# Moving the back transforms, the sums and the feed-forward within the two-row steps of a window-attention and Fourier kernel

## The chip, the cores and the metric

The kernel runs on one core of a Trainium2 chip. The metric is the device time of the whole kernel in microseconds: 3787.6 us before the change, the median of three runs (3779.0 to 3789.97). All data are float32.

## What is computed

Two layers on 32 images of 56 x 56 tokens with 128 channels. Each layer adds a branch of the group-normalised image to the image:

```python
x = x + window_attention(gn(x))     # 7x7 windows, shifted by 3, 4 heads, relative bias and mask
x = x + feedforward(fourier(gn(x)))
# fourier: along rows and along columns, cosine transform, keep 32 modes,
#          one 128x128 matrix per mode, transform back; the two results are added
# feedforward: relu(h @ W1 + b1) @ W2 + b2, 128 -> 512 -> 128
```

`gn` takes mean and variance over a whole image for each group of 4 channels, so the second layer of an image starts when its attention is over.

## The kernel before

**Image and rows.** An image has 8 rows of windows (`NWR`), of 8 windows with 49 tokens each. After the first 8 rows, which run one by one (`first_rows`), everything runs in `step(g)`, which takes two rows: `cur` are the rows 2g and 2g+1, `prev` the two before them. An image thus takes four steps (`STEPS`), and 32 images take 128 steps and a tail.

**A step's attention.** For `cur`: queries and keys (`attn_qk`, L322 to L342), scores (`attn_scores`: 16 matmuls of each row into two PSUM banks, L376, then two additions of bias and mask on VectorE, L384), maximum and subtraction (`attn_max`, L394 and L395), values of the tokens (`attn_v`, L354 and L361), exponential (`attn_exp`, L401). For `prev`, in the step after: sums and division (`attn_divide`, L406 to L409), transposes of the weights on TensorE (`attn_transpose`, L420: two banks for each row, the first copied to `aT` by VectorE, L430, the second by ScalarE, L428), weights times values (`attn_values`, L445, two banks, copied by L476 on VectorE and L478 on ScalarE), projection and residual (`attn_project`, L487 and L495, written to the scratch tensor `scr`). `attn_sums` takes the sums for the second normalisation of the rows before those: first L509 on VectorE, and after its `yield` the squares on ScalarE (L517) and their sums on VectorE (L518).

**A step's second layer.** Image b enters it at step g = 4b + 5 (`CONV_BEGIN` = 5), and d counts its steps from there. `fourier(g)` lists the images at work with their d: two of them, the newest at d = 0 to 3 and the one before at d = 4 to 7.
- d = 0: statistics (`fourier_stats`: L529 adds up all sums of the image on VectorE, L538 is a matmul on them, L546 to L569 are small operations on VectorE with one on GpSimd, L567), all four forward transforms along the width and two along the height (`transform`, L596 and L604).
- d = 1: two more along the height, the modes of the width (`mix`, L630, L638, through the DRAM scratch `zscr`).
- d = 2: the modes of the height; transform back along the width, four groups of 16 lines (the last has 8) (`load_modes`, then `modes_back`: L669 into two banks, copied by L680 on ScalarE and VectorE).
- d = 3: transform back along the height, four groups; here both banks are added to `xf` by VectorE (L685).
- d = 4 to 7 (`FF_BEGIN` = 4): feed-forward, eight groups of 384 tokens (the last has 448), two in a step. `ff_in` loads the residual, multiplies by W1 (L717, four banks) and takes the relu on ScalarE (L725, `hid`), `ff_out` multiplies by W2 (L737) and adds the residual on VectorE (L746).

**The next image** is brought in meanwhile: `image_group` (eight of them; L260 on TensorE, L270 on ScalarE, L271 on VectorE, L275 on GpSimd): three before the transposes of the step with d = 1, three at its end and two at the beginning of the step with d = 2. `image_norm`, a generator in four pieces, takes the statistics of the next image (L282 to L313), with small matmuls (L285, L298, L311), VectorE in between (L291, L293, L300, L304) and GpSimd for the power (L302). Its second matmul, L298, is in the step with d = 2 ahead of the transposes.

**Order.** The body is built under `tc.manual_schedule(engines={PE, Activation, DVE, Pool})`: each of these four engines takes its instructions in the order in which the program writes them down. What an instruction waits for, across engines, is worked out from the tiles that it touches. Two PSUM pools of four banks each go round: `pa` for attention, `image_group`, `image_norm` and `fourier_stats`, `pc` for transforms, modes and feed-forward. An allocation takes the bank that was given out four allocations earlier, so the first matmul into it waits for the copy out of it.

Of the kernel before, what the change touches and what calls it, by code (L numbers as in the profile page):

```python
# [41 lines left out]
FF_GROUPS = (3 * P,) * 7 + (7 * JP,)  # L42
# [5 lines left out]
def swin_fourier_kernel(  # L48
# [564 lines left out]
    def load_columns(im, g):  # L613

        t = work.tile([TC, CH, C], F32, tag="htok", name="htok", bufs=2)
        src = im.scr.rearrange("h (n r) c -> r h n c", r=2)
        for r in range(2):
            nc.sync.dma_start(t[r * S : (r + 1) * S], src[r, :, CH * g : CH * (g + 1)])
        im.cols[g] = t
# [28 lines left out]
    def load_modes(im, width, g):  # L648
        l0, n = LINES[g]
        zT = work.tile([P, 4, C], F32, tag="zT", name="zT", bufs=4)  # L650
        nc.sync.dma_start(
            zT[:, : n // 4],
            im.zscr[width][l0 : l0 + n].rearrange("(m r) u k c -> (r u k) m c", r=4),
        )
        im.zT[width, g] = zT
# [120 lines left out]

    images = {}
    STEPS = NWR // 2
    FF_BEGIN = 4

    def row(r):
        return (images[r // NWR], r % NWR) if 0 <= r < NB * NWR else (None, 0)
# [4 lines left out]
    def fourier(g):  # L787

        b, d = divmod(g - CONV_BEGIN, STEPS)
        return [(images[b - k], d + k * STEPS) for k in (1, 0) if 0 <= b - k < NB]  # L790

    first_done = set()

# [4 lines left out]
    def step(g):  # L798
        prev, cur, b, i = rows(g - 1), rows(g), *divmod(g, STEPS)
        conv = fourier(g)  # L800
        following = images.get(b + 1)

        def groups(js):
            if following:
                for j in js:
                    image_group(following, j)

        norm = None
        if following and i == STEPS - 1:
            norm = image_norm(following)  # L810


        if i == STEPS - 1:
            groups((6, 7))
        if norm:
            next(norm)
        for im, d in conv:
            if d >= FF_BEGIN:
                ff_in(im, 2 * (d - FF_BEGIN))
        for im, j, r in prev:  # L820
            if once("divide", r):
                attn_divide(r)
        sums = []
        for im, j, r in rows(g - 2):
            if once("sums", r):
                sums.append(attn_sums(im, j))
                next(sums[-1])
        for im, j, r in cur:
            attn_qk(im, j, r, False)
        if norm:  # L830
            next(norm)
        for k in sums:
            next(k)
        for im, d in conv:
            if d == 0:
                im.stats = fourier_stats(im)
                im.cols = {}
                next(im.stats)
                load_columns(im, 0)
                load_columns(im, 1)  # L840
            if d in (2, 3):
                for k in range(len(LINES)):
                    load_modes(im, d == 2, k)
        for im, d in conv:
            if d >= FF_BEGIN:
                ff_out(im, 2 * (d - FF_BEGIN))
                ff_in(im, 2 * (d - FF_BEGIN) + 1)
        for im, d in conv:
            if d == 0:
                next(im.stats)  # L850
        if norm:
            next(norm)
        if i == STEPS - 2:
            groups((0, 1, 2))
        for im, j, r in prev:
            attn_transpose(im, j, r)


        for im, j, r in prev[:1]:
            attn_values(im, j, r)  # L860


        for k in range(2):
            for im, d in conv:
                if d in (2, 3):
                    modes_back(im, d == 2, k)
        for im, j, r in cur:
            attn_scores(im, j, r)
        for k in range(2, 4):
            for im, d in conv:  # L870
                if d in (2, 3):
                    modes_back(im, d == 2, k)
        for im, j, r in cur:
            attn_max(r)


        for im, d in conv:
            if d == 0:
                for k in range(4):
                    transform(im, True, k)  # L880
            if d in (0, 1):
                for k in (2 * d, 2 * d + 1):
                    transform(im, False, k)
                    if d == 0:
                        load_columns(im, k + 2)
            if d in (1, 2):
                for k in range(4):
                    mix(im, d == 1, k)
        for im, j, r in cur:
            attn_v(im, j, r)  # L890


        for im, j, r in prev[1:]:
            attn_values(im, j, r)


        for im, j, r in cur:
            attn_exp(r)
        for im, d in conv:
            if d >= FF_BEGIN:  # L900
                ff_out(im, 2 * (d - FF_BEGIN) + 1)
        for im, j, r in prev:
            attn_project(im, j)
        if i == 1 and b + 1 < NB:
            images[b + 1] = image_begin(b + 1)
        if i == STEPS - 2:
            groups((3, 4, 5))
        if norm:
            next(norm)
# [125 lines left out]
```

## Time and profile before

| | before |
|---|---|
| device time, us | 3787.6 (3779.0 to 3789.97) |
| span of the profiled execution, us | 3778.7 |
| TensorE matmul: busy | 3612.5 us, 96% |
| TensorE weight load: busy | 3055.2 us, 81% |
| VectorE: busy | 2280.0 us, 60% |
| ScalarE: busy | 2155.6 us, 57% |
| GpSimd: busy | 1366.0 us, 36% |
| share of TensorE in the chain that ended last | 84% |
| DMA: mean rate | 103 GB/s |

Busy time is the time in which an engine executes. A matmul of float32 counts twice here, since it is executed as two passes; the end of a matmul is modelled. In the profile's lines, "pa<-aT,v" says that `pa` is written and `aT` and `v` are read; what stands after "<-" in brackets or in the wait view released the engine from its idle time. `L420` is line 420 of the kernel. PE is TensorE, PEld its weight load, ACT ScalarE, DVE VectorE, POOL GpSimd.

### The profile page before, as it was taken

To read this page: it belongs to the slowest core of one execution; us is meant where nothing else is said; L and a number is where in the kernel's file an instruction comes from. 1 tells how busy PE (TensorE), PEld (TensorE's weight loads), DVE (VectorE), ACT (ScalarE), POOL (GpSimd) and SP (SyncE) were. 2 spreads that over 40 slices of the span, in tenths; PEclk is the share of its full clock that TensorE was granted. 3 is DMA by queue.
4 is the path that set the end of the run, shared out by engine and by line. 5 is a ranking of instruction groups with operands and counts; after the bars stand their busy time and mean duration, and the time that the engine had idled before them with its cause. 6 is when DMAs were issued, how large, how long until landed. Compare 5 with 4: busy or idle time off the path is not lost.

```text
span 3778.7 us, 140104 instructions
## 1 busy us (share of the span) xinstructions
PE 3612.5 (96%) x61696; PEld 3055.2 (81%) x61696; DVE 2280.0 (60%) x4739; ACT 2155.6 (57%) x3913; POOL 1366.0 (36%) x1453
## 2 busy tenths in 40 slices
PE   7899999999999999999999999999999999999999
PEld 5788888888887888888888788878888888888887
DVE  6766566665665656665656656566566666565641
ACT  5565555655555555556555565555555555555553
POOL 5343333433333333333333333333343333333321
PEclk9999999999999999999999999999999999999999
DMA  4343333434434344344433343443444333434333
GB/s 111 93 112 99 98 94 101 120 98 111 106 92 105 96 114 105 92 106 117 98 97 104 93 118 99 113 101 92 105 102 114 98 100 102 114 98 104 95 105 96
DMA packets 688417, 388.93 MB, mean 103 GB/s; under 512 B 41120, under 2 KB 658753, under 8 KB 687553
## 3 DMA queue, kind: packets, MB, share of 16 engines
q1 hardware_dynamic: 687197, 379.65, 38.8%
q8 instruction: 485, 7.95, 0.9%
q14 instruction: 124, 1.01, 0.1%
q10 hardware_dynamic: 611, 0.32, 0.0%
HBM read 218.29 MB, written 161.48 MB: 101 GB/s over the span
## 4 chain that ended last, share of the span: by engine, by line
PE 84%; DVE 7%; ACT 4%; issue 3%; SPq 1%; DMA 1%; POOL 0%; ACTq 0%; DVEq 0%; POOLq 0%
PE pc L737 18%; PE pc L717 15%; PE pc L630 6%; PE pc L596 6%; PE pa L354 6%; PE pa L376 5%; PE pa L487 5%; PE pa L445 5%; PE pc L669 4%; PE pa L329 4%; PE pa L322 4%; PE pa L420 3%; ACT hid L725 2%; PE pa L260 2%; DVE st L271 1%
## 5 line engine op out<-in xcount | busy, mean ns | idle before, releaser
L725 ACT ACTIVATE hid<-pc,b1sb 128x384 f32<-128x384 f32 (+1 forms) x1024 | 600.3, 587 | 610.4 <-PE pc L717 557.2
L737 PE MATMUL pc<-wff,hid 128*128 128x128 f32 x6400 | 783.3, 278 | 8.0 <-issue 7.3
L737 PEld LDWEIGHTS pc<-wff,hid 128*128 128x128 f32 x6400 | 745.4, 190 | 52.6 <-issue 8.7
L717 PE MATMUL pc<-xf,wff 128*128 128x384 f32 (+1 forms) x2048 | 727.0, 496 | 19.8 <-DVE res L746 19.8
L395 POOL TENSOR_TENSOR a<-a,mx 128x784 f32<-128x784 f32 x256 | 383.8, 1520 | 1000.0 <-DVE mx L394 906.9
L409 POOL TENSOR_TENSOR a<-a,rs 128x784 f32<-128x784 f32 x256 | 383.6, 1521 | 611.7 <-ACT hid L725 369.2
L717 PEld LDWEIGHTS pc<-xf,wff 128*128 128x128 f32 x2048 | 367.0, 190 | 243.9 <-DVE res L746 37.7
L476 DVE TENSOR_SCALAR oT<-pa,bqkv 128x98 f32<-128x98 f32 (+2 forms) x768 | 171.1, 278 | 500.9 <-PE pa L445 500.9
L275 POOL TENSOR_TENSOR xl<-xl,bproj 112x384 f32<-112x384 f32 (+1 forms) x256 | 291.3, 1141 | 282.0 <-PE pa L260 277.1
L746 DVE TENSOR_TENSOR res<-pc,res 128x384 f32<-128x384 f32 (+1 forms) x288 | 148.1, 523 | 375.6 <-PE pc L737 208.5
L707 POOL TENSOR_TENSOR res<-res,b2sb 128x384 f32<-128x384 f32 (+1 forms) x288 | 270.4, 944 | 263.3 <-DMA res<-scr 254.9
L604 ACT ACTIVATE y<-pc,rstd 128x448 f32<-128x448 f32 x256 | 167.5, 655 | 195.6 <-PE pc L596 189.7
L384 DVE TENSOR_TENSOR a<-pa,bm 128x392 f32<-128x392 f32 x512 | 256.2, 558 | 36.1 <-PE pa L376 31.4
L361 ACT COPY v<-pa 128x512 f32<-128x512 f32 x256 | 147.8, 589 | 201.8 <-PE pa L354 201.3
L376 PE MATMUL pa<-k,q 64*64 64x98 f32 x8192 | 231.4, 248 | 32.7 <-issue 27.8
L445 PE MATMUL pa<-aT,v 49*32 49x49 f32 x16384 | 208.7, 212 | 49.5 <-DVE aT L430 40.2
L354 PE MATMUL pa<-wn,xw 128*64 128x128 f32 x4096 | 250.2, 274 | 2.8 <-DVE a L384 2.8
L401 ACT ACTIVATE a<-a 128x784 f32<-128x784 f32 x256 | 210.8, 864 | 70.1 <-POOL a L395 70.1
L342 DVE TENSOR_SCALAR k<-pa,heads,bqkv 128x392 f32<-128x392 f32 x248 | 169.2, 684 | 134.8 <-ACT k L334 134.8
L445 PEld LDWEIGHTS pa<-aT,v 49*32 49x32 f32 x16384 | 174.5, 105 | 89.1 <-ACT aT L428 50.8
L376 PEld LDWEIGHTS pa<-k,q 64*64 64x64 f32 x8192 | 200.5, 132 | 50.4 <-issue 36.6
L406 DVE TENSOR_REDUCE sm<-a 128x16 f32<-128x784 f32 x256 | 238.1, 930 | 4.4 <-ACT a L401 4.4
(90 smaller groups left out, 5903.3 us busy)
## 6 DMA issues: line engine op xcount, KB each, us to landing
zscr<-z SPq DMA_DIRECT2D x512, 112.0 KB
htok<-scr SPq DMA_DIRECT2D x256, 196.0 KB
res<-scr SPq DMA_DIRECT2D x256, 192.0 KB
zT<-zscr SPq DMA_DIRECT2D x192, 256.0 KB
out_dram<-res SPq DMA_DIRECT2D x224, 192.0 KB
scr<-xl SPq DMA_DIRECT2D x128, 224.0 KB
xl<-in_x_dram SPq DMA_DIRECT2D x32, 784.0 KB
xl<-in_x_dram SPq DMA_DIRECT2D x32, 672.0 KB
```

Of the source, the lines that this page charges most:

```text
L275: nc.gpsimd.tensor_tensor(piece, piece, bproj.unsqueeze(1).to_broadcast([TC, n1 - n0, C]), ALU.add)
L354: nc.tensor.matmul(pv[hs, j * C : (j + 1) * C], lhsT=im.xw[i][:, w * WT : w * WT + JP], rhs=im.w[:, 2 * C : 3 * C], start=True, stop=True,)
L376: nc.tensor.matmul(ps[hp][HALVES[e], pr * 2 * WT : (pr + 1) * 2 * WT], lhsT=q[cs, w * WT : w * WT + JP], rhs=k[cs, :, w], start=True, stop ...
L384: nc.vector.tensor_tensor(a[:, 2 * hp : 2 * hp + 2, :, 0:WT].rearrange("p u w j -> p w u j"), ps[hp][:, :RT].rearrange("p (w u j) -> p w u ...
L395: nc.gpsimd.tensor_tensor(a3, a3, mx.unsqueeze(2).to_broadcast([P, 2 * NWR, WT]), ALU.subtract)
L406: nc.vector.tensor_reduce(sm, a3, axis=AX.X, op=ALU.add)
L409: nc.gpsimd.tensor_tensor(a3, a3, rs.unsqueeze(2).to_broadcast([P, 2 * NWR, WT]), ALU.mult)
L445: nc.tensor.matmul(po4[u][h * HD : (h + 1) * HD, 2 * f + e], lhsT=v[ks, 2 * f + e, h * HD : (h + 1) * HD], rhs=im.aT[i][f][ks, h, e * JP : ...
L707: nc.gpsimd.tensor_tensor(res[:m, c0:c1], res[:m, c0:c1], b2sb[:m].unsqueeze(1).to_broadcast([m, c1 - c0, C]), ALU.add,)
L717: nc.tensor.matmul(ph[:, :n], lhsT=wff1[:, f * P : (f + 1) * P], rhs=xff[:, t0 : t0 + n], start=True, stop=True,)
L725: nc.scalar.activation(hf[:, :n], ph[:, :n], AF.Relu, bias=b1sb[:, f : f + 1])
L737: nc.tensor.matmul(pf[:m, c * C : (c + 1) * C], lhsT=im.hid[f][:, c * P : c * P + m], rhs=wff2[:, f], start=(f == 0), stop=(f == NF - 1),)
```

## The change

All of it is in the planning of the steps; no operation is added or taken out.

1. The transforms back are spread over four steps instead of two: two groups at each of d = 2 and 3 for the width and d = 4 and 5 for the height. One group stands ahead of the scores of `cur`, one behind them; before, two stood on each side.
2. The values of the first row of `prev`, which followed the transposes directly, follow the scores and the second group back, so that matmuls that do not depend on the copies of the transposes lie between.
3. The feed-forward begins at d = 6 instead of 4, since the transforms back now end at d = 5. Three images can be in the second layer at once, and the last two steps of one run beside the first two of the image after the next one.
4. The DMA loads of a step (columns of `scr` at d = 0, modes at d = 2 to 5) are issued ahead of the feed-forward in the middle of the step.
5. `ff_out` and the second `ff_in` stand ahead of the second half of `attn_sums` (`next(k)`: L517 and L518); before, they stood behind it.
6. The statistics at d = 0: the sum L529 still follows the second half of `attn_sums`, and so follows the feed-forward now; the second half (L538 and after) stands behind the transposes instead of before them.

```diff
-    FF_BEGIN = 4
+    FF_BEGIN = 6
...
-        return [(images[b - k], d + k * STEPS) for k in (1, 0) if 0 <= b - k < NB]
+        return [
+            (images[b - k], d + k * STEPS)
+            for k in (2, 1, 0)
+            if 0 <= b - k < NB and d + k * STEPS < FF_BEGIN + len(FF_GROUPS) // 2
+        ]
...
+        for im, d in conv:
+            if d == 0:
+                im.cols = {}
+                load_columns(im, 0)
+                load_columns(im, 1)
+            if 2 <= d < FF_BEGIN:
+                for k in range(2):
+                    load_modes(im, d < 4, d % 2 * 2 + k)
+        for im, d in conv:
+            if d >= FF_BEGIN:
+                ff_out(im, 2 * (d - FF_BEGIN))
+                ff_in(im, 2 * (d - FF_BEGIN) + 1)
         for k in sums:
             next(k)
         for im, d in conv:
             if d == 0:
                 im.stats = fourier_stats(im)
-                im.cols = {}
-                next(im.stats)
-                load_columns(im, 0)
-                load_columns(im, 1)
-            if d in (2, 3):
-                for k in range(len(LINES)):
-                    load_modes(im, d == 2, k)
-        for im, d in conv:
-            if d >= FF_BEGIN:
-                ff_out(im, 2 * (d - FF_BEGIN))
-                ff_in(im, 2 * (d - FF_BEGIN) + 1)
-        for im, d in conv:
-            if d == 0:
                 next(im.stats)
...
         for im, j, r in prev:
             attn_transpose(im, j, r)
+        for im, d in conv:
+            if d == 0:
+                next(im.stats)
+
+        def back(k):
+            for im, d in conv:
+                if 2 <= d < FF_BEGIN:
+                    modes_back(im, d < 4, d % 2 * 2 + k)
+
+        back(0)
+        for im, j, r in cur:
+            attn_scores(im, j, r)
+        back(1)
 
         for im, j, r in prev[:1]:
             attn_values(im, j, r)
-
-        for k in range(2):
-            for im, d in conv:
-                if d in (2, 3):
-                    modes_back(im, d == 2, k)
-        for im, j, r in cur:
-            attn_scores(im, j, r)
-        for k in range(2, 4):
-            for im, d in conv:
-                if d in (2, 3):
-                    modes_back(im, d == 2, k)
         for im, j, r in cur:
             attn_max(r)
```

## The prediction

> **What bounds the kernel now.** I read the totals first, then the waits of TensorE, then one image's four steps as windows, then those steps engine by engine in the timeline.
>
> The totals of the page:
>
> ```profile
> PE 3612.5 (96%) x61696; PEld 3055.2 (81%) x61696; DVE 2280.0 (60%) x4739; ACT 2155.6 (57%) x3913; POOL 1366.0 (36%) x1453
> ```
>
> TensorE sets the time: 166 of 3778.7 us are left. The granted clock was 0.996. No reordering can win more than those 166 us, and it can lose any amount, since a TensorE idle for lack of an operand has nothing to make it up with. The wait view of TensorE says what they are (engine line waited for: us in total, times, longest us):
>
> ```profile
> PE pa L445 <- DVE aT L430: 40.2, 61, 1.4
> PE pa L376 <- issue: 27.8, 37, 1.6
> PE pc L717 <- DVE res L746: 19.8, 29, 0.7
> ...
> PE pc L630 <- ACT xf L680: 4.2, 19, 0.2
> ```
>
> The attention values (L445) wait for the transposed weights; L717, on 29 steps, for a bank that L746 empties. "issue" is time for which the profile shows no partner. Now one image from the middle, one window a step (columns: stretch, length, busy time of PE, PEld, DVE, ACT, POOL, clock, DMA), each from the start of its transposes (L420):
>
> ```profile
> 1481.38:1510.04 28.66, 27.84 (x509) 23.93 (x509) 15.10 (x33) 17.90 (x33) 9.30 (x11) 1.00 0.61 129
> 1510.04:1540.65 30.61, 29.48 (x473) 25.27 (x471) 20.58 (x41) 18.75 (x35) 16.34 (x21) 1.00 0.33 95
> 1540.65:1569.20 28.55, 28.31 (x507) 24.01 (x506) 16.60 (x35) 17.55 (x34) 8.91 (x8) 1.00 0.40 116
> 1569.20:1594.60 25.40, 25.40 (x449) 21.32 (x448) 18.80 (x38) 12.89 (x23) 7.95 (x6) 1.00 0.32 82
> ```
>
> I call them steps 0 to 3, after d of the newest image. The idle time of TensorE in this image is 2.2 us: 0.82 and 0.46 before L445 in steps 0 and 1, 0.67 before L717 and 0.24 before L630. Step 3 has none. The timeline shows why (start, us, what):
>
> ```profile
> 1476.73 1.03 ACT L517 ACTIVATE sq<-xl 112x384 f32<-112x384 f32 x2
> 1479.53 2.52 ACT L725 ACTIVATE hid<-pc,b1sb 128x384 f32<-128x384 f32 x4 [1.78 <-PE pc L717]
> 1482.41 0.54 ACT L428 COPY aT<-pa 113x452 f32<-113x452 f32 x1 [0.36 <-PE pa L420]
> ```
>
> ```profile
> 1483.14 0.16 DVE L569 SCALAR_TENSOR_TENSOR shift<-ms,rstd 128x1 f32<-128x1 f32 x1 [0.66 <-POOL rstd L567]
> 1483.22 1.16 DVE L430 COPY aT<-pa 113x452 f32<-113x452 f32 x2
> ...
> 1505.07 1.14 DVE L518 TENSOR_REDUCE part<-sq 112x32 f32<-112x384 f32 x2
> 1506.48 0.56 DVE L746 TENSOR_TENSOR res<-pc,res 128x384 f32<-128x384 f32 x1 [0.28 <-issue]
> 1510.06 1.50 DVE L271 BATCH_NORM_STATS2 st<-xw 128x6 f32<-128x392 f32 x3 [3.02 <-ACT xw L270]
> 1511.48 1.15 DVE L430 COPY aT<-pa 113x452 f32<-113x452 f32 x2
> ```
>
> ```profile
> 1483.99 0.80 PE L445 MATMUL pa<-aT,v 49*32 49x49 f32 x64 [0.82 <-DVE aT L430]
> ```
>
> In step 0 VectorE's copy L430 stands behind the statistics (L546 to L569, 1481.58 to 1483.30), in step 1 behind three L271. The first copy ends at 1483.84, and L445 starts 0.15 later: my price of a hand-over to TensorE. Equally important: the squares L517 stand on ScalarE *before* the four relus (L725), in an idle stretch, and so L518 is over before the transposes begin. The last relu ends 0.84 us after the ff_in matmuls (1482.05 against 1481.21; the same in step 3, 1570.04 against 1569.20).
>
> **What the Trainium skill says.** "PSUM — Partial Sum Buffer", section "Engine vs sequencer instructions": the queues of ScalarE, VectorE and GpSimd are strict FIFO, and matmuls start in program order. The trace agrees: L430 of 1511.48 sat behind L271 although its transposes had begun at 1510.04. "Perfetto Trace Analysis", section "Identifying the Most-Contended Engine": matmul busy share is no good measure of closeness to the roofline. Here PEld, 81%, points to TensorE as well. Same page, "Optimization Strategy": a bubble that repeats can mean too few buffers for the next tile. That bears on what follows: the four transposes take all four `pa` banks, and the scores need two of them back.
>
> **The change, part by part.** Each engine's order is that of the program, so I place every instruction behind those ahead of it. T is when TensorE reaches the transposes, as it does now.
>
> *Removed.* Scores and one `modes_back` group now lie between transposes and values, so L445's old wait goes (40.2), L746 moves ahead of L518, so L717's goes (19.8), and only two groups stand ahead of `mix`, so L630's goes (4.2). Together 64 us.
>
> *Moved at no cost.* No TensorE work is added. Loads of zT are still issued a step or more after their writes. The feed-forward's delay keeps its two groups a step; softmax (L394 to L409) starts up to 4 us later, but its exp waits behind the second values on ScalarE anyway (L401 at T+13.1 in step 0) and its division ends more than 6 us before the next transposes.
>
> *Added: `next(k)` after the second ff_in.* It puts L517 behind the relus: last relu T+0.84, squares to T+1.87 (1.03), L518 to T+2.6 (its second takes 0.68 after the second square). The first copy L430 then ends at T+3.15 (0.62), and the second at T+3.7. Before, step 3's first copy ended at T+1.23. Transposes take 1.62 us of issue, one back group 0.85 (1.70 for two), a row's scores 0.88 (1.77 for two), two score additions 1.0 (1.99 for four).
> - Step 3: transposes to T+1.62, back(0) to 2.5. Scores need the bank of the first copy, 3.15+0.15 = 3.3: wait 0.8. Values find their two banks some 0.1 late. Together **0.85**.
> - Step 2: the norm's L300 and L304 stand behind L518 too. L300 at T+2.55 frees the bank of the last transpose, which has started by 1.2: wait 1.5. L304 follows 0.82 later (measured, through GpSimd's L302), the copy ends at 3.9, scores at 4.05 after back(0) to 3.95: 0.1. **1.6**.
> - Step 1: ff_in is over 1.23 earlier, but L270 (0.42 each) also stands behind the squares: it ends at 1.1, 1.5 and 1.9, and the last transposes end at 2.4 instead of 1.62: 0.8. Three L271 (1.5) then L430: first copy 3.4, scores 3.55 against back(0) to 3.25: 0.3. Additions end at 6.1, values are reached at 5.65: 0.6. **1.7**.
> - Step 0: the total L529 (0.69) follows L518, to T+3.2, and L538, now directly after the transposes, needs it: TensorE waits from 1.62 to 3.35, 1.7. Queued behind it are back(0), scores and everything else. Statistics end at 5.95 (chain of 1.72 after the copies), two additions of back(0) at 7.0 (1.11), scores' at 8.0. Values are reached at 6.9, start at 8.15: 1.25. **2.95**.
>
> Sum: 29 of steps 0 and 1 each, 30 of 2 and 3 have both attention and feed-forward: 29 x (2.95+1.7) + 30 x (1.6+0.85) = 208 us added. Net of the 64: +144.
>
> *Feed-forward two steps later.* Image 0 runs steps 0 and 1 once more without it. Its absence at 110 to 157 us shows waits of 1.26, 1.41 and 4.88, against 0.83, 0.46 and 0.67 with it: +5.6. At the end four more groups have nothing between ff_in and ff_out: L737 takes 3.17 there, 2.92 in the mean elsewhere, +1. Together +6.
>
> *Unknown: "issue".* It comes in clusters, at L376 above all. The trace does not say what it depends on. A wait ahead of the scores may cover it: between none and all 78 us that the clusters cost (the excess of all steps over their clean lengths); other arrangements of short matmuls could add 30. I take half of L376's: -14.
>
> 3787.6 + 144 + 6 - 14 = 3924.
>
> **Rivals.**
> 1. *Late copies, as above*: 3924, chance 0.6. For it: each term is a queue position times a measured duration. Against it: hand-built schedules of five queues leave room for a bank assigned otherwise.
> 2. *The same, but the new waits swallow the "issue" clusters, or a third of them fails to appear*: 144 becomes about 66 to 96: 3854 to 3890, chance 0.24. For: both are idle TensorE. Against: many clusters lie later in the step.
> 3. *As the order of matmuls suggests*: scores and back groups cover the copies fully, nothing new arises: -64 + 6 = 3730, chance 0.12. For: in step 3 of now, copies, two back groups and scores run with no wait. Against: there L518 was done 3 us before.
> 4. *Both cancel*: 3788, chance 0.04.
>
> **How the numbers follow.** Slower 0.84 (rivals 1 and 2), same 0.04, faster 0.12. The range goes from the lower half of rival 2 (3835, where half the L538 term fails besides) to 3970 (208 us in full, nothing of "issue" saved and 30 added: 3968).
>
> **What would show it.** L517 after L725 on ScalarE, with L518 ending 2 to 3 us after the transposes start; a wait of TensorE at L538 for L529, near 1.7 us in each step 0; waits of L376 for L430, near 0.8 in step 3; waits of L420 for L270 in step 1 and for L300 in step 2; L445 waiting for L384. The waits for L746 and L680 gone. I am wrong if L538 and L376 show no such waits, or if L517 runs between the relus and ends early.

## The result and the profile after

| | before | after |
|---|---|---|
| device time, us | 3783.3 (3778.67 to 3789.97, 4 runs) | 3849.78 (3845.89 to 3852.51, 4 runs) |
| span of the profiled execution, us | 3778.7 | 3850.2 |
| TensorE idle in the span, us | 166.2 | 204.4 |
| granted clock in the span | 0.996 | 0.992 |

The change makes the kernel slower: 1.0174 times the time before, with a 95% interval of 1.0151 to 1.0196. That is +66 us; the forecast was +136. The kernel moved to the side that the forecast named, but by about half of the distance.

The totals of the profile page after:

```profile
PE 3645.8 (95%) x61696; PEld 3078.4 (80%) x61696; DVE 2260.3 (59%) x4739; ACT 2143.3 (56%) x3913; POOL 1364.3 (35%) x1453
```

No engine has one instruction more, and TensorE's busy time is 33 us longer all the same. The other part of the 71.5 us by which the span grew is 38 us of idle time. The wait view of TensorE after:

```profile
PE pa L538 <- DVE tot L529: 52.0, 32, 3.1
PE pa L420 <- DVE ve L300: 30.4, 29, 1.1
PE pa L445 <- DVE a L384: 24.1, 71, 1.1
PE pa L445 <- issue: 17.0, 21, 2.0
PE pa L420 <- ACT xw L270: 13.4, 28, 0.7
...
PE pa L376 <- DVE aT L430: 7.5, 34, 1.0
```

Every new wait of the forecast is there with the releaser named in it: the statistics' matmul L538 for the total L529 (step 0), the transposes L420 for L300 (step 2) and for L270 (step 1), the values L445 for the additions L384 (steps 0 and 1), the scores L376 for the copy L430 (step 3). The three old waits (L445 for L430, L717 for L746, L630 for L680; 64 us together) are not in the view any more. The new ones are 52.0 + 30.4 + 24.1 + 13.4 + 7.5 = 127 us of idle time; the forecast said 208.

Windows of one image in the middle, after, as the prediction cut them, by the starts of L420: steps 0, 1 and 2, then the whole image (stretch, length, busy time of PE, PEld, DVE, ACT, POOL, clock, DMA):

```profile
1474.85:1507.54 32.69, 30.17 (x573) 25.59 (x572) 17.80 (x38) 18.02 (x33) 9.71 (x12) 1.00 0.53 115
1507.54:1540.28 32.74, 31.95 (x528) 27.48 (x527) 22.08 (x46) 18.59 (x36) 16.36 (x21) 1.00 0.31 90
1540.28:1568.25 27.97, 26.92 (x459) 22.95 (x458) 15.47 (x33) 16.35 (x33) 8.50 (x7) 1.00 0.35 102
1474.85:1591.43 116.58, 112.03 (x1929) 95.01 (x1928) 70.30 (x147) 66.45 (x123) 42.52 (x45) 1.00 0.40 102
```

Before, such an image took 113.22 us with 2.2 idle. Now it takes 116.58 with 4.55 idle: 2.52 of it in step 0 (first length minus first busy time), 0.79 in step 1, 1.05 in step 2. So two thirds of the loss in an image are idle time, and 1.0 us is longer busy time for the same matmuls.

Where the waits come from stands in the timeline of a step 0 (T = 1591.73, the start of the transposes). First ScalarE, then VectorE, then TensorE:

```profile
1590.06 2.52 ACT L725 ACTIVATE hid<-pc,b1sb 128x384 f32<-128x384 f32 x4 [2.71 <-PE pc L717]
1592.47 1.03 ACT L517 ACTIVATE sq<-xl 112x384 f32<-112x384 f32 x2
```

```profile
1593.02 1.20 DVE L518 TENSOR_REDUCE part<-sq 112x32 f32<-112x384 f32 x2 [3.06 <-ACT sq L517]
1594.26 0.69 DVE L529 TENSOR_REDUCE tot<-part 112x64 f32<-112x512 f32 x1
1594.86 1.16 DVE L430 COPY aT<-pa 113x452 f32<-113x452 f32 x2
...
1598.64 1.97 DVE L384 TENSOR_TENSOR a<-pa,bm 128x392 f32<-128x392 f32 x4
```

```profile
1591.73 1.75 PE L420 MATMUL pa<-ident,a 113*113 113x113 f32 x16
1595.09 0.41 PE L538 MATMUL pa<-tot,gmean 112*128 112x64 f32 x2 [1.61 <-DVE tot L529]
1595.43 1.00 PE L669 MATMUL pc<-idcth,zT 64*64 64x112 f32 x32
1596.24 1.53 PE L376 MATMUL pa<-k,q 64*64 64x98 f32 x64
1597.59 0.95 PE L669 MATMUL pc<-idcth,zT 64*64 64x112 f32 x32
1599.25 0.27 PE L445 MATMUL pa<-aT,v 49*32 49x49 f32 x2 [0.71 <-DVE a L384]
1599.72 0.79 PE L445 MATMUL pa<-aT,v 49*32 49x49 f32 x62 [0.20 <-DVE a L384]
```

The reader is to follow one thread downwards. The squares (L517) stand behind the relus (L725) and begin 0.74 after T. VectorE has been idle for 3.06 us when the first square is done, and L518, L529 and L430 follow each other without a gap. L538 is next in TensorE's queue after the transposes and waits 1.61 us for L529. The additions L384 come last on VectorE, behind the statistics and the copies of the back group, and the values wait for them. The experiments will show that this last wait, unlike the first, is there without the late squares too.

### The profile page after: what moved, and what is told of

It reads as the page before. It is cut to its first block, busy times and chain, and to the rows that moved or that the text cites. A ratio compares the mean times of both kernels' runs of the same rounds, so it can differ in the third digit from the quotient of the medians.

```text
span 3850.2 us, 139915 instructions
## 1 busy us (share of the span) xinstructions
PE 3645.8 (95%) x61696; PEld 3078.4 (80%) x61696; DVE 2260.3 (59%) x4739; ACT 2143.3 (56%) x3913; POOL 1364.3 (35%) x1453
## 4 chain that ended last, share of the span: by engine, by line
PE 81%; DVE 8%; ACT 6%; issue 3%; SPq 1%; DMA 1%; POOL 0%; ACTq 0%; DVEq 0%; POOLq 0%
PE pc L737 19%; PE pc L717 14%; PE pc L630 6%; PE pa L354 6%; PE pc L596 6%; PE pa L487 5%; PE pa L445 5%; PE pa L322 4%; PE pa L376 4%; PE pa L329 4%; ACT hid L725 4%; PE pc L669 4%; DVE part L518 3%; ACT sq L517 2%; PE pa L420 2%
## 5 line engine op out<-in xcount | busy, mean ns | idle before, releaser
L725 ACT ACTIVATE hid<-pc,b1sb 128x384 f32<-128x384 f32 (+1 forms) x1024 | 601.3, 588 | 698.1 <-PE pc L717 644.3
L717 PE MATMUL pc<-xf,wff 128*128 128x384 f32 (+1 forms) x2048 | 719.3, 494 | 0.0
L717 PEld LDWEIGHTS pc<-xf,wff 128*128 128x128 f32 x2048 | 369.2, 190 | 214.1 <-issue 36.0
L746 DVE TENSOR_TENSOR res<-pc,res 128x384 f32<-128x384 f32 (+1 forms) x288 | 148.5, 525 | 512.7 <-PE pc L737 305.0
L518 DVE TENSOR_REDUCE part<-sq 112x32 f32<-112x384 f32 (+1 forms) x256 | 154.0, 620 | 350.8 <-ACT sq L517 350.8
L478 ACT ACTIVATE oT<-pa,bqkv 128x196 f32<-128x196 f32 x256 | 116.5, 455 | 373.4 <-PE pa L445 360.0
L420 PE MATMUL pa<-ident,a 113*113 113x113 f32 x2048 | 245.4, 268 | 47.7 <-DVE ve L300 30.4
L420 PEld LDWEIGHTS pa<-ident,a 113*113 113x113 f32 x2048 | 226.1, 180 | 78.5 <-DVE ve L300 35.6
L445 PE MATMUL pa<-aT,v 49*32 49x49 f32 x16384 | 229.5, 211 | 46.0 <-DVE a L384 24.1
L445 PEld LDWEIGHTS pa<-aT,v 49*32 49x32 f32 x16384 | 183.9, 105 | 100.4 <-DVE a L384 45.6
L384 DVE TENSOR_TENSOR a<-pa,bm 128x392 f32<-128x392 f32 x512 | 253.2, 558 | 1.1 <-PE pa L376 1.0
L376 PE MATMUL pa<-k,q 64*64 64x98 f32 x8192 | 227.1, 255 | 10.7 <-DVE aT L430 7.5
```

The source lines that it names most:

```text
L376: nc.tensor.matmul(ps[hp][HALVES[e], pr * 2 * WT : (pr + 1) * 2 * WT], lhsT=q[cs, w * WT : w * WT + JP], rhs=k[cs, :, w], start=True, stop ...
L420: nc.tensor.transpose(pt[:PW, h * P : h * P + PW], a[:PW, h, 2 * hf : 2 * hf + 2].rearrange("p w j -> p (w j)")[:, :PW], ident[:PW, :PW],)
L445: nc.tensor.matmul(po4[u][h * HD : (h + 1) * HD, 2 * f + e], lhsT=v[ks, 2 * f + e, h * HD : (h + 1) * HD], rhs=im.aT[i][f][ks, h, e * JP : ...
L518: nc.vector.tensor_reduce(im.part[:, 1, :, i], sq.rearrange("p n (g c) -> p g n c", c=4), axis=AX.XY, op=ALU.add,)
L717: nc.tensor.matmul(ph[:, :n], lhsT=wff1[:, f * P : (f + 1) * P], rhs=xff[:, t0 : t0 + n], start=True, stop=True,)
L725: nc.scalar.activation(hf[:, :n], ph[:, :n], AF.Relu, bias=b1sb[:, f : f + 1])
```

## The experiments

Each run has its own runs of the kernel before on the same chip, with medians of 3781.6 to 3789.4 us, and its ratio is taken to those. For the accounting I use two numbers beside the time. The *shortest image* is the sum over the four kinds of steps of the second-shortest length over the 28 images in the middle; it is 113.23 us before and 116.54 after. The *excess* is by how much those 28 images together are longer than 28 shortest ones: 80 us before, 45 after. The clusters of "issue" are in the excess, and so is what is lost where the clock is lower. Both numbers come from one profile of each kernel.

### Are the late squares the cause?

Theory: part 5 of the change, the second half of the sums behind the feed-forward, makes the new waits at L538, L420 and L376, and the rest of the change is a gain. Rival: the new order of back transforms, scores and values itself brings a loss, so that the kernel stays slower than before with early sums.

**sums_ahead** is the changed kernel with the second half of the sums (L517 and L518) back where it was:

```diff
+        for k in sums:
+            next(k)
         for im, d in conv:
...
                 ff_in(im, 2 * (d - FF_BEGIN) + 1)
-        for k in sums:
-            next(k)
```

> The changed kernel with one line group moved back: the second half of the sums (squares L517, their sums L518) stands ahead of ff_out and the second ff_in again, as before the change. Late squares (my theory): the waits of TensorE for L529 at L538 (52.0 us), for L300 (30.4) and L270 (13.4) at L420 and for L430 at L376 (7.5) go to under 10 us in all; L717 waits for L746 again, some 20 us as before the change; issue waits may come back to some 50 us. 3740 to 3785 us. Rival (the new arrangement itself, three images at once or values behind the scores, costs the time): it stays above 3820 us.

Measured: 3736.99 us (3724.99 to 3738.37), ratio 0.9862 [0.9842, 0.9883]; shortest image 112.52. Its wait view:

```profile
PE pa L445 <- DVE a L384: 21.4, 86, 1.0
PE pc L717 <- DVE res L746: 19.9, 29, 0.7
PE pa L445 <- issue: 18.3, 30, 1.6
...
PE pa L538 <- DVE tot L529: 2.0, 2, 1.0
```

The changed kernel becomes faster than the kernel before, even 3 us faster than the expected range, and the waits at L538, L420 and L376 are gone but for 2.0 us at L538 and 1.4 at L376. But the old wait of L717 for L746 is back: L746 again stands behind L518 on VectorE. So part 5 did remove that wait, by means that cost more than it. The values' wait for the additions stays, 21.4 us of 24.1: it is not the late squares that make it.

**squares_ahead** takes only what was needed of part 5. The generator of the sums gets one more `yield`, so that L517 stands ahead of the feed-forward and L518 stays behind L746 (behind this line, line numbers are one higher):

```diff
         nc.scalar.activation(sq, piece, AF.Square)
+        yield
         nc.vector.tensor_reduce(
...
+        for k in sums:
+            next(k)
         for im, d in conv:
```

> The changed kernel with the squares L517 alone moved ahead of ff_out and the second ff_in; their sums L518 stay behind L746. Late squares on ScalarE (my theory): L518 finds its operand ready, ends before the transposes begin, and both the new waits and the wait of L717 for L746 are gone: 10 to 25 us less than the run with squares and sums ahead, 3725 to 3770 us. Rival (L518's place on VectorE, not that of L517 on ScalarE, makes the copies late): within 15 us of the changed kernel, near 3850 us.

Measured: 3703.69 us (3696.41 to 3709.34), ratio 0.9780 [0.9761, 0.9799]; shortest image 111.56. This is faster than both kernels, by 84 and 146 us, and by 33 than `sums_ahead`, where 10 to 25 were expected. Its page totals and VectorE in a step 0 with T = 1544.35:

```profile
PE 3603.6 (97%) x61696; PEld 3049.3 (82%) x61696; DVE 2274.3 (61%) x4739; ACT 2160.4 (58%) x3913; POOL 1364.5 (37%) x1453
```

```profile
1542.50 1.14 DVE L519 TENSOR_REDUCE part<-sq 112x32 f32<-112x384 f32 x2
1543.67 0.69 DVE L530 TENSOR_REDUCE tot<-part 112x64 f32<-112x512 f32 x1
1544.95 0.63 DVE L430 COPY aT<-pa 113x452 f32<-113x452 f32 x1 [0.59 <-PE pa L420]
```

The total L530 (L529 of the other kernels) is over 0.01 us after T, 3.21 us earlier in its step than after, and VectorE now waits for the transposes instead of the reverse. The span is 143 us shorter than that of after: 101 us less idle time and 42 us less busy time, with the same matmuls. L445 still waits 20.7 us for L384.

**sums_late_alone** does the opposite: the kernel before, with the sums' second half and the statistics that need it put behind the second `ff_in`, and nothing else.

```diff
-        for k in sums:
-            next(k)
         for im, d in conv:
             if d == 0:
-                im.stats = fourier_stats(im)
                 im.cols = {}
-                next(im.stats)
...
                 ff_in(im, 2 * (d - FF_BEGIN) + 1)
+        for k in sums:
+            next(k)
+        for im, d in conv:
+            if d == 0:
+                im.stats = fourier_stats(im)
+                next(im.stats)
```

> The kernel before with only the sums' second half (and L529, which needs them) moved behind the second ff_in; values directly behind the transposes, feed-forward at d = 4, transforms back as before. Late squares: the transposes wait for L270 and L300, L538 for L529, and L445 for the copy L430 in all four steps, about 1.3 us each; 5 us an image more in sum: 3890 to 3980 us. Rival (the order of the sums is harmless, the other parts cost): 3775 to 3800 us.

Measured: 4046.48 us (4040.43 to 4053.7), ratio 1.0688 [1.0666, 1.0709]; shortest image 120.50. Its wait view:

```profile
PE pa L538 <- DVE tot L529: 103.4, 32, 4.5
PE pa L445 <- DVE aT L430: 100.3, 98, 1.5
PE pa L420 <- DVE ve L300: 30.4, 29, 1.1
...
PE pa L420 <- ACT xw L270: 12.0, 29, 0.4
```

In the old order the late squares cost +258 us, and 7.27 us in the shortest image; in the new order they cost 116.54 − 112.52 = 4.02. The waits for L300 and L270 are the same in both. The difference lies where the new order puts work in between: L538 directly behind the feed-forward waits twice as long (103.4 against 52.0), and L445 directly behind the transposes pays 100.3 for L430, where the new order pays 7.5 at the scores and 24.1 at the values. So the spread order does hide waits, as it was meant to. The run is 66 us above the expected range, and not all of its +258 us are waits: the granted clock of this run is 0.970, against 0.996 before, and TensorE's busy time is 97 us longer (3709.0). As an estimate, 0.030 of 4049 us less 0.004 of 3779 us, up to 106 us of the +258 go with the clock; the second-shortest lengths leave it out. When the clock falls is told in the last section.

The theory stands for the four waits at L538, L420 and L376, 103 of the 127 us, and its rival falls. The fifth, of L445 for L384, belongs to the new place of the values (part 2), as `values_at_once` below shows.

### Which of the other waits matter?

**stats_behind_scores**: the changed kernel with the second half of the statistics behind the second back group, so that L538 has the scores ahead of it.

```diff
-        for im, d in conv:
-            if d == 0:
-                next(im.stats)
...
         back(1)
+        for im, d in conv:
+            if d == 0:
+                next(im.stats)
```

> The changed kernel (squares late) with the second half of the statistics (L538 to L569) behind the scores and back(1) instead of directly behind the transposes. The wait of L538 for L529 (52.0 us) goes. My theory: the copies L430 stand behind L518 and L529 all the same, so the scores wait for them instead, about 1.3 us in each step 0, and 15 to 30 us are won: 3820 to 3838 us. Rival (L538 alone is the loss in step 0, and its whole wait is won): 3795 to 3805 us.

Measured: 3820.5 us (3818.56 to 3827.69), ratio 1.0079 [1.0063, 1.0096]. Its wait view:

```profile
PE pa L376 <- DVE aT L430: 37.3, 65, 1.2
PE pa L420 <- DVE ve L300: 30.4, 29, 1.1
PE pa L445 <- issue: 19.3, 25, 3.1
```

L538 hardly waits any more (1.4 us), and the values' wait for L384 falls from 24.1 to 6.3, but only 29 us are won: the scores' wait for L430 grows from 7.5 to 37.3, since the copies still stand behind the late sums. Another instruction of TensorE now waits for the same late work.

**values_at_once** is `sums_ahead` with the first row's values directly behind the transposes again, which undoes part 2:

```diff
+        for im, j, r in prev[:1]:
+            attn_values(im, j, r)
+
         back(0)
...
         back(1)
 
-        for im, j, r in prev[:1]:
-            attn_values(im, j, r)
         for im, j, r in cur:
```

> The run with squares and sums ahead, with one more edit: the values of the first row stand directly behind the transposes again (in step 0 behind L538), ahead of back(0). It tells what moving the values is worth, and whether it is what lowered the issue waits. In that run the steps' excess over their shortest lengths was 43 us over 28 images, before the change 81. If the values' place makes the issue waits: the excess returns to 70 to 90 us and L445 waits for L430 some 40 us: 3770 to 3800 us. If the spreading of the transforms back makes them: the excess stays at 35 to 55, only L445 for L430 comes: 3745 to 3765 us.

**squares_ahead_values_at_once** is the same edit on `squares_ahead`.

> The run with the squares ahead, with the values of the first row directly behind the transposes again. Moving them made no difference where squares and sums were both ahead (3736 and 3737 us), and the wait of L717 that the squares' place saves is elsewhere: 3695 to 3712 us. If the values' place matters once nothing else waits: 3720 us or more.

Measured: 3735.91 us (3732.33 to 3739.68) against the 3736.99 of `sums_ahead`, and 3710.44 (3705.89 to 3720.57) against the 3703.69 of `squares_ahead`. Both pairs overlap; the expectation had `values_at_once` slower, at 3745 us or more. In place of the 21.4 us for L384, the wait view of `values_at_once` has `PE pa L445 <- DVE aT L430: 16.5, 30, 1.4`. With early sums it makes no difference that can be measured whether the values stand early or late: one wait takes the place of another of about the same size.

**additions_first** tries to win the 20.7 us that L445 still waits for L384 in `squares_ahead`. The copies of the first back group (L680, L685) are written behind the scores' additions, by a `yield` in `modes_back`:

```diff
+        yield
         for li in range(2):
...
-        back(0)
+        first = back(0)
+        for t in first:
+            next(t)
         for im, j, r in cur:
             attn_scores(im, j, r)
-        back(1)
+        for t in first:
+            next(t, None)
+        for t in back(1):
+            next(t)
+            next(t, None)
```

> The run with the squares ahead, with one more edit: the copies of back(0) stand behind the additions of the scores (L384) on VectorE instead of ahead of them. What is left in that run is L445 waiting for L384, 20.7 us. If the copies of back(0) are what delays the additions: 8 us or less of it stay, 10 to 22 us less time, 3680 to 3697 us. If the statistics (step 0) and L271 (step 1) delay them: no change, 3700 to 3710 us.

Measured: 3714.38 us (3709.28 to 3725.06), ratio 0.9800 [0.9777, 0.9822]; no gain over `squares_ahead`, and above both expectations. L445 waits only 1.7 us for L384 now, but the first line of its wait view (L597 is L596 of the changed kernel, L687 its L685) is

```profile
PE pc L597 <- DVE xf L687: 26.6, 49, 0.7
```

The forward transforms of the same step take `pc` banks that the postponed copies were to empty. The wait has moved from one pool to the other.

### What the rest of the change is worth alone

**ff_later_alone** is the kernel before with part 3 only: `FF_BEGIN = 6` and the list of up to three images.

> The kernel before with the feed-forward two steps later (d = 6) and nothing else; images with d = 4 and 5 do nothing. My theory: only start and end pay, 5 to 15 us: 3788 to 3800 us. Rival (three images at once, or the longer life of scr and xf, costs in every image): 3830 us or more.

Measured: 3790.86 us (12 runs, 3789.19 to 3803.48), ratio 1.0007 [0.9994, 1.0021]: −2 to +8 us. The forecast had +6 for it.

**spread_alone** adds to that the back transforms, one group on each side of the scores in four steps (part 1, with their loads); values, sums and statistics stay as before:

```diff
+        def back(k):
             for im, d in conv:
-                if d in (2, 3):
-                    modes_back(im, d == 2, k)
+                if 2 <= d < FF_BEGIN:
+                    modes_back(im, d < 4, d % 2 * 2 + k)
+
+        back(0)
         for im, j, r in cur:
             attn_scores(im, j, r)
-        for k in range(2, 4):
...
+        back(1)
```

> The run with the feed-forward two steps later alone (3790.9 us, excess over the shortest lengths 85 us in 28 images) with one more edit: the transforms back at one group on each side of the scores in four steps, instead of two in two. Values, sums and statistics stay as in the kernel before. If spreading these short matmuls lowers the instruction-fetch waits: the excess falls to 40 to 60 us, the old waits of L445 for L430 (some 41 us) and of L717 for L746 (20) stay, 3745 to 3770 us. If the statistics' or the loads' place lowered them: the excess stays near 80, 3780 to 3795 us.

**stats_behind_alone** is the kernel before with the second half of the statistics (L538 to L569) behind the transposes and nothing else; **spread_and_stats_behind** has the edits of both.

```diff
-        for im, d in conv:
-            if d == 0:
-                next(im.stats)
         if norm:
...
             attn_transpose(im, j, r)
+        for im, d in conv:
+            if d == 0:
+                next(im.stats)
```

> The kernel before with one edit: the second half of the statistics (L538 to L569) stands behind the transposes instead of ahead of them; sums, values, transforms back and feed-forward as before. If the statistics' place is what lowers the instruction-fetch waits: the excess of the steps over their shortest lengths, 80 us in 28 images, falls to 40 to 60 us, and the wait of L445 for L430 in step 0 (0.82 each, 25 us) goes too: 3720 to 3745 us. If their place and the spread of the transforms back are needed together: only the 25 us go, 3755 to 3770 us.

> The run with the transforms back spread alone (3779.7 us, excess 84 us) with one more edit: the second half of the statistics behind the transposes. It differs from the run with squares and sums ahead and the values at once (3735.9 us, excess 53) in the order of L529 and L746 alone. If the statistics' place lowers the excess: 40 to 60 us, 3725 to 3745 us. If it was the loads' place or chance: 75 us or more, 3755 to 3765 us.

| | us | ratio, 95% | shortest image | excess |
|---|---|---|---|---|
| spread_alone | 3779.72 (18 runs) | 0.9970 [0.9958, 0.9982] | 112.60 | 84 |
| stats_behind_alone | 3757.54 (4 runs) | 0.9938 [0.9901, 0.9975] | 113.18 | 57 |
| spread_and_stats_behind | 3740.64 (2 runs) | 0.9883 [0.9843, 0.9922] | 112.21 | 61 |

The spread by itself is worth 0.3%, as its second expectation had it: the wait view of `spread_alone` still has the values waiting for the copies.

```profile
PE pa L445 <- DVE aT L430: 40.2, 59, 1.4
PE pa L376 <- issue: 31.5, 34, 1.8
PE pc L717 <- DVE res L746: 20.0, 29, 0.7
```

```profile
PE pa L376 <- issue: 21.9, 30, 1.3
PE pc L717 <- DVE res L746: 20.3, 29, 0.9
PE pa L376 <- DVE oT L476: 17.3, 31, 0.6
PE pa L445 <- DVE aT L430: 15.5, 31, 1.4
```

The second fence is the wait view of `stats_behind_alone`. With the copies ahead of the statistics on VectorE, L445's wait shrinks from 40.2 to 15.5 us, but 17.3 come back at the scores, and the shortest image stays what it was (113.18). What was won, 24 us, is in the excess (80 to 57). The same 23 us show between `spread_alone` and `spread_and_stats_behind` (84 to 61). In both pairs some 21 us of it lie in step 0, where the statistics stand. So the excess fell as the first expectation for `stats_behind_alone` had it, but the time did not, since of the 25 us at L445 most came back at the scores. This leads to the last question.

### What is "issue"?

The forecast credited 14 us, on the thought that a wait ahead of the scores may cover the clusters. The excess fell by 36 us, and all "issue" waits of TensorE from 51.8 to 25.4 us. `sums_ahead` speaks against the thought: without the new waits its excess is 43, its "issue" waits 26.8 us. So most of the fall goes with the new order of the matmuls. `sums_late_alone`, with more waits than any other, decides nothing: its excess is 120, but up to 103 us of that are lost in stretches of half clock, if half of each stretch is counted (5 us in the kernel before, 19 after), and its "issue" waits are 39.1 us.

**load_split_before** tests whether the bulk load of the next image disturbs TensorE. It is the kernel before with the second half of each image's load (672 KB) issued one step later than the first half.

```diff
+        if following and i == 2 and b:
+            load_part(following.x, b + 1, NCH // 2, NCH)
         norm = None
```

> The kernel before, with the second half of the next image's load (672 KB) issued at the start of the step after, not together with the first half. If the issue waits are instruction fetches behind the bulk load of that step: the excess of all steps over their shortest lengths falls from 81 us (28 images) to 50 or less, 3745 to 3765 us. If they depend on the order of matmuls alone: 3780 to 3795 us.

Measured: 3788.22 us (12 runs), ratio 1.0001 [0.999, 1.0013]; excess 81, and "issue" at the scores 28.4 us against 27.8. Moving half of the load changes nothing, so the load is hardly the cause.

The page's list of DMA queues has one for instructions. Before it reads

```profile
q8 instruction: 485, 7.95, 0.9%
```

(packets, MB, share). 7.95 MB in 485 packets are 16.4 KB each. The excess of the 28 images before has a period of about six images, which nothing in the program has. If TensorE's instructions come in blocks of a fixed number and a dense stretch of short matmuls can outrun them, the stretch that is hit shifts from image to image by what is left over. Two runs change that remainder: in the kernel before, **pe_6_more** writes 6 of the L445 matmuls of each image's row with i = 3 twice, **pe_54_more** writes 54 more. Each such matmul is two matmul and two weight-load instructions, so an image has 24 or 216 more.

```diff
+EXTRA = 6
...
+        again = EXTRA if i == 3 else 0
+        order = [(f, e, h, u) for f in range(2) for e in range(2) for h in range(NH) for u in range(2)]
+        order = [o for k, o in enumerate(order) for _ in range(1 + again // 32 + (k < again % 32))]
+        for f, e, h, u in order:
```

> The kernel before, with six matmuls of the values (L445 there) written down twice in one row of each image: the output stays the same, TensorE has 24 instructions more in an image (two passes, each with its weight load), 0.15 us. In the kernel before the issue waits come in clusters 24 steps (6 images) apart, and the instruction queue moves 485 blocks of 16 KB for 123392 TensorE instructions, so an image is about 3880 instructions of 64 bytes, 15 blocks and 40 instructions. If a cluster is a place of the block borders relative to the steps: the drift becomes 64 instructions an image and the clusters come 16 steps apart (4 images). If it is something else in the DMA traffic or the clock: 24 steps as before. Time 3783 to 3800 us either way.

> The same with 54 matmuls written down twice: 216 instructions more in an image, 1.3 us of work, 40 us in all. Block borders: the drift becomes about 256, that is none, so clusters of 24 steps disappear: steps of one kind last nearly the same from image to image, all disturbed or none. Something else: clusters as before. 3800 to 3850 us.

Measured: 3800.45 us (ratio 1.0039 [1.0023, 1.0054], excess 88) and 3829.52 us (2 runs, 1.0116 [1.0096, 1.0136], excess 48; here the shortest image itself is 2.5 longer, all of it in the step with the added matmuls, for which the expectation had 1.3). The queue lines of the two:

```profile
q8 instruction: 488, 8.00, 0.9%
```

```profile
q8 instruction: 512, 8.39, 0.9%
```

32 x 24 = 768 instructions more are 3 packets more, and 32 x 216 = 6912 are 27 more: 256 to a packet both times. 485 packets of 256 are 3880 in each image, which is 15 packets and 40 instructions; the left-over 40 comes round in 256/40 = 6.4 images, 64 in exactly 4, and 256 at once. The excess of image after image (us):

```
before      2.7 7.2 4.1 0.8 1.2 0.3  2.9 7.8 3.8 0.7 1.2 0.0  1.9 4.5 5.1 5.2 0.9 0.2  3.4 5.4 4.6 3.5 0.7 0.1  1.8 2.8 4.9 1.7
pe_6_more   4.8 0.9 0.1 5.0  5.0 1.2 1.0 4.8  5.7 0.8 1.3 8.0  3.9 1.4 1.9 4.7  2.9 1.4 1.5 9.4  3.9 0.0 3.1 4.0  0.6 0.0 7.0 4.2
pe_54_more  2.3 1.9 2.0 2.3 2.4 2.1 2.2 1.8 1.7 2.0 2.2 1.7 2.4 1.4 1.9 2.1 1.7 1.3 0.9 1.6 0.8 1.3 0.8 1.3 1.4 1.3 1.1 1.4
```

A period of about six, one of four, and none; with none, the loss does not go but is much the same in each image. That the clusters follow the position in the instruction stream is shown; that the wait is for the arrival of a block is what I conclude from it. Why the place of the statistics takes 23 us from the excess stays open: it adds no instruction, so the remainder stays 40.

## Why the prediction was right in its mechanism and wrong in its size

**What held.** The direction, the cause (squares behind relus), each of the five waits with both ends named, and the old waits gone with their 64 us. One cause was wrong: the forecast put the values' wait for the additions down to the late squares, and the runs show 21 us of it without them. This wait stands in the place of the 40.2 us for L430, so less than 64 us was really won. The Trainium skill's statement in "PSUM — Partial Sum Buffer", section "Engine vs sequencer instructions", that these queues are strictly first in, first out, carried the whole derivation, and the traces agree: in `squares_ahead` L517 takes another place in ScalarE's queue, with the same 1.03 us for the two, and 146 us go.

**What failed: the term of 208 us for new waits.** As idle time they measured 127. The four sums of the forecast against the gaps that the image after and its steps show:

| step | forecast, us | shown, us |
|---|---|---|
| 0: L538 for L529 | 1.7 | 1.61 |
| 0: values for the additions | 1.25 | 0.71 + 0.20 |
| 1: L420 for L270 | 0.8 | 0.47 |
| 1: scores; values | 0.3; 0.6 | 0; 0.20 |
| 2: L420 for L300 | 1.5 | 1.05 |
| 2: scores | 0.1 | 0 |
| 3: scores for L430, values | 0.85 | 0.19 |
| sum | 7.1 | 4.43 |

Idle time is not the whole of a delay. `squares_ahead` differs from the changed kernel in the place of L517 alone; from the one to the other, the second-shortest steps 0 to 3 grow by 2.21, 0.99, 1.30 and 0.49 us, where the forecast added 2.95, 1.7, 1.6 and 0.85. Over its 29 and 30 images this is 147 us for 208.

By this measure the first wait of a step was priced well in steps 0 and 1: the work behind it, back(0), starts 1.83 us later in step 0 (forecast 1.7) and 0.77 later in step 1 (0.8). The second waits behind it failed: the values start only another 0.38 and 0.22 us later, where the forecast had 1.25 and, with the scores, 0.9. Part of the reason is above: without the late squares the values would have waited too. In step 2 the first wait was 1.30 for 1.5, in step 3 about 0.4 for 0.8. Three errors of the working can be seen in the traces. Step 3 after shows the first two (T = 1568.42; ScalarE, VectorE, TensorE):

```profile
1566.69 2.52 ACT L725 ACTIVATE hid<-pc,b1sb 128x384 f32<-128x384 f32 x4 [2.59 <-PE pc L717]
1569.10 1.03 ACT L517 ACTIVATE sq<-xl 112x384 f32<-112x384 f32 x2
```

```profile
1570.77 1.16 DVE L430 COPY aT<-pa 113x452 f32<-113x452 f32 x2
```

```profile
1570.92 0.34 PE L376 MATMUL pa<-k,q 64*64 64x98 f32 x4
1571.45 1.48 PE L376 MATMUL pa<-k,q 64*64 64x98 f32 x58 [0.19 <-DVE aT L430]
```

- *Durations were added end to end.* The squares begin at 1569.10 while the relus end at 1569.21; in step 0, L430 begins 0.09 before L529 ends. Each link of the chain relu, squares, sums, copy is up to 0.1 us shorter than its duration. The first copy ends at T+2.97 and not at T+3.15, its hand-over to TensorE took 0.06 and not 0.15, and the first scores that need the copied bank start at T+3.03 and not at T+3.3.
- *A group of matmuls was taken to need all of its banks at once.* Four matmuls of L376 start on the bank already free, and in step 0 two of L445 start when the first of their banks is; their time comes off the wait. Less comes off than it seems: four scores take about 0.08 us in a running group, the records count 0.34 as busy, and only the 0.19 after them as idle.
- *The work ahead of a wait was given its old length.* In the step 0 shown, 64 scores between two back groups start 1.35 us before the group behind them; the forecast used 1.77. (Between two back groups in step 3 of the kernel before, they take 1.35 as well.) This goes the other way (the values are reached sooner), and yet the values start at T+7.52 and not at T+8.15, since the first error is larger over the longer chain.

A smaller reading was wrong without effect: the division ends 3.4 to 6.5 us before the next transposes in the kernel before, not more than 6 in each step.

**The other terms.** The feed-forward's +6 holds within what can be measured (−2 to +8). The −14 for "issue" had the right sign and too small a size; its reason is not borne out by `sums_ahead`. The shortest image grew by 3.31 us, where the forecast's net was 4.9; the windows of the image shown split such a growth into 2.36 of idle time and 1.0 of busy time for the same matmuls, of which the forecast did not speak.

**The sum.** The 3.31 us are −1.67 for all but the late squares (113.23 to 111.56) and +4.98 for the late squares (to 116.54). Over 28 images they make +92.8 us; the excess is −35.8; the start and the end, with the images there, +14.5. Together 71.5, the difference of the two spans. The forecast's own rival 2 (3854 to 3890, its lower end without the +6 of the feed-forward) came nearest, though by another route: no wait failed to appear; most were smaller.

Divided by parts, the error lies in part 5. For all the others the forecast had −40.2 − 4.2 + 6 − 14 = −52 us, and `sums_ahead` measured −51; that is luck, since the values' wait of 21 us was not in this sum and the excess fell by 38 instead of 14. For part 5 the forecast had 208 − 19.8 = +188, and the step from `sums_ahead` to the changed kernel is +113.

## What to carry to other kernels

When an instruction is moved to free what stands behind it, ask of each of its halves which engine's queue it sits in: here VectorE's sums had to go behind L746, but ScalarE's squares, written by the same call, had to stay in the idle stretch ahead of the relus, and splitting the two was worth 146 us against moving both and 33 against moving neither. To size a wait by hand, take starts from the trace and not sums of durations, since neighbours on an engine overlap in the records and the first matmuls of a group need only their own bank. Ask of each second wait behind a first one whether it would be there anyway; the sum made without this gave 208 us, where 147 came. And before work is put between a producer and its consumer, see whether the banks and copies of that work come back as a wait of the same size elsewhere, as they did in five of these runs.

## What the runs showed of the hardware that was not expected

- TensorE's instructions arrive in packets of 256 (768 more gave 3 packets, 6912 gave 27), and TensorE, at the scores above all, loses time that follows the position in this stream: 48 to 88 us of excess in the kernels with the order of before, up to 10 of it by the clock, with a period set by the number of instructions in an image modulo 256.
- Idle time of TensorE is not all that a wait costs. Between `squares_ahead` and after, 42 us of the 143 are longer busy time for the same matmuls. As an estimate, 15 of these go with the lower clock (0.996 to 0.992 of 3646). The rest stands where the new waits are: in the 28 images, L376 in step 3, L420 in steps 1 and 2 and L538 are busy for 32 us more, and other groups for some 7 us less. Ahead of such a wait the record of the last matmul (0.24 us long, where the next ones start 0.07 apart in a running group of scores) is counted as busy to its end.
- The clock falls by half, in stretches of 3.4 us or a multiple of that. The windows of the same 64 scores in two images after, at full clock and at half (the third number from the end), are

```profile
1479.36:1480.71 1.35, 1.35 (x72) 1.35 (x68) 0.62 (x5) 0.00 (x0) 0.55 (x1) 1.00 0.00 0
771.34:773.95 2.61, 2.61 (x72) 2.61 (x68) 1.91 (x7) 0.00 (x0) 0.55 (x1) 0.50 0.02 6
```

  In the 28 images after, each of the 11 such stretches begins within 1.2 us after the end of a wait of TensorE of 1.6 us or more, nine of them that of L538; before, there are three, behind waits of 1.56, 2.32 and 3.50 us. Most of the 28 waits of L538 are followed by none. The order with most gaps had the lowest granted clock (`sums_late_alone`, 0.970, against 0.992 to 0.998 in the runs named here). That the waits are the cause is not shown.
- Consecutive instructions on ScalarE and on VectorE overlap by about 0.1 us in the records (1569.10 against 1569.21; 1594.86 against 1594.95).
